# Merging the transfers of y and of the expert biases in a planned two-layer kernel, with a new searched order

## The chip, the cores and the metric

The kernel runs on one core of one Trainium2 chip. The core has five engines that run their own instruction queues: TensorE (PE in the profile, with its weight loads as PEld), VectorE (DVE), ScalarE (ACT), GpSimd (POOL) and SyncE (SP). In this kernel SP does nothing but issue the DMA transfers. Sixteen DMA engines move the data. The metric is the device time of one execution in microseconds (us), as the median of several runs. Before the change it is 741.02 us, from three runs of 740.77 to 742.02 us.

## The reference

What is computed is a chain of six residual blocks on x of shape (8, 256, 128), all in float32. The first and the third block are the same soft mixture of experts (16 experts with 64 slots each); the change touches only what feeds them.

```python
def _L0_ffn_ref(x, norm_g, norm_b, slot_g, slot_b, scale, slot_embeds, Wg, bg, Wu, bu, Wd, bd):
    x = _layernorm(x, norm_g, norm_b)
    se = _layernorm(slot_embeds, slot_g, slot_b) * scale
    logits = jnp.einsum('bnd,esd->bnes', x, se)
    dispatch = jax.nn.softmax(logits, axis=1)
    combine = jax.nn.softmax(logits.reshape(x.shape[0], x.shape[1], -1), axis=-1)
    slots = jnp.einsum('bnd,bnes->besd', x, dispatch)
    gate = jax.nn.gelu(jnp.einsum('besd,edf->besf', slots, Wg) + bg[None, :, None, :], approximate=False)
    up = jnp.einsum('besd,edf->besf', slots, Wu) + bu[None, :, None, :]
    eout = jnp.einsum('besf,efo->beso', gate * up, Wd) + bd[None, :, None, :]
    eout = eout.reshape(eout.shape[0], -1, eout.shape[-1])
    return jnp.einsum('bns,bso->bno', combine, eout)

...
x = x + 0.5 * _L0_ffn_ref(_layernorm(x, axis=-1), ...)
x = x + _L0_attn_ref(_layernorm(x, axis=-1), ...)
x = x + 0.5 * _L0_ffn_ref(_layernorm(x, axis=-1), ...)
x = x + 0.5 * _L1_ffn_ref(_layernorm(x, axis=-1), ...)
x = x + _L1_attn_ref(_layernorm(x, axis=-1), ...)
x = x + 0.5 * _L1_ffn_ref(_layernorm(x, axis=-1), ...)
```

## The kernel before, in words

**How the work is laid out.** The eight batches form two groups of four. For each group the function `group` runs, for two layers: `dispatch` for each of the four batches (the softmax over tokens and the gathering of the slots), `experts` for all four batches together, and then `combine` batch by batch; after the first layer comes `linear`, the linear attention. Then come `glu`, `favor` and `glu` again. So there are 16 dispatches and 4 passes over the 16 experts in all. The second group is planned behind the first by the constant `BEHIND` (L241), so that one group's experts and the other group's dispatches are done at the same time.

**What sets the order.** Nothing is issued at once. Each piece of work is a `Step` with a cost per engine, the cells that it reads and writes, and the buffers that it takes. `Plan.place` (L123) then simulates the engines: among all steps that could start, it takes the one with the earliest start, and breaks ties by a key. The key is shifted part by part by the 202 numbers of `SHIFTS` (L16), which were found by a search. A step is ready when the steps that it needs have ended, plus a latency for the engine (`LAG`, L74; 2000 ns for SP) and an extra `lag` that the step states itself. Buffers are limited: 4 of kind `we` for expert weights, 4 of kind `k4` (which the replicated y uses among others), 10 of kind `comb`. `Plan.issue` (L205) writes the instructions out in the planned order of starts, one queue per engine, so on the chip each engine works through its own fixed list and waits where data are not there. Where the plan finds TensorE idle for over 700 ns, `idle` (L1397) puts in dummy matmuls (L1399), to keep its clock up.

**The work that the change touches.** `replicated` (L573) is called by each dispatch. The gather matmuls (L691) want the normalized y in a layout in which the tokens of one quarter lie on 32 partitions and are repeated on each of the four groups of 32 partitions. To get it, `spill` (L577) writes y to a DRAM tensor `spilled[b]` of shape (32, 8, 128) in four DMAs (L579), one per quarter of the partitions, 32 KB each; `spread` (L584) reads that tensor back four times (L586), 128 KB each, once into each group of 32 partitions. `fetch` (L760) in `experts` loads the weights of one expert into a `we` buffer of 128 rows of 896 numbers: 768 weights (L764, 384 KB), and for every even expert the output biases of this expert and of the next into the last 128 columns, in two DMAs (L767), 32 KB each, every one repeating a row of 128 numbers over 64 partitions. `biased` (L829) adds them after the down projection (L818). A fetch has two conditions: the slots of the third dispatch of its group have been started (`(sl, "in", BG - 2, 0)`), and a `we` buffer is free, which is so when the down projection of an earlier pair of experts has ended.

**Other transfers that the new lengths touch.** `squares_turned` (L440) transposes a tile by way of DRAM: one DMA out (L449) and four DMAs back (L455) that put the 32x32 squares where they belong. Their planned lengths change, not the DMAs.

**The other steps named later.** L615 logits, L632 their running maximum, L649 and L657 the maximum and the exponentials of the dispatch, L670 the division on POOL, L678 the transposes in squares on DVE, L495/L493 the copies of gathered slots into place, L737 and L743 the exponentials for the combination, L787 gate and up projections of the experts, L793 and L798 their activation and product, L859 the combination, L928 to L995 linear attention.

Of the kernel before, what the change touches and what calls it, by code (L numbers as in the profile page):

```python
# [13 lines left out]
P = 128  # L14

SHIFTS = (  # L16
    -2751, -1692, -1691, -12195, -784, -1588, -17523, -441, -1660, -895, -929, -659, -543, -591,
    -517, -633, -219, -357, -610, -370, -144, -340, -138, -261, -103, -124, -149, -112, -87,
    328, -365, -173, -179, -134, 14, 40, -32, 136, -182, -43, -162, -672, 13, -20, 26, 13, -393,
    -13, -49, 76, 108, 25, -337, -106, -98, -405, -124, -14, 106, -15, -91, -232, -26, -141, 72,  # L20
    179, -149, -60, -56, -94, -291, -910, -397, 168, -109, -149, -2, -601, -150, 12, -21, -762,
    -20, -100, 231, -63, -522, -971, -639, -490, -1134, 34, -143, -240, -1126, 30, 98, 272,
    -229, -245, 48, 535, -647, -666, -418, 7, 144, -282, -73, 220, 168, 36, -1118, -353, -720,
    -886, -200, -34, 24, 100, 11, -24, 70, 30, -50, -121, 47, 25, 9, -51, 143, -939, -125, -300,
    -662, -491, -371, -203, -437, -21, -285, -479, -125, 412, 243, 49, 284, 369, 566, -147,
    -339, 157, 267, -173, -269, 162, -518, -492, 53, 116, -414, -523, -222, -451, -400, -304,
    -82, 145, -77, -134, -36, -467, -865, -141, -372, -407, -524, -134, 12, 58, -154, 246, 41,
    -111, 22, 62, -756, -131, 38, -435, -1331, -683, -948, -2046, -2339, -2000, -3450, -2514,
    -3516, -3317, -2307, -1684,
)  # L30


# [184 lines left out]
def macaron_kernel(ctx: ExitStack, tc: tile.TileContext, i: dict, out: bass.AP):  # L217
# [10 lines left out]
    nc = tc.nc  # L228
    B, N, D = out.shape
    TT = N // P  # L230
    NT = B * TT
    E, S, F = 16, 64, 256
# [6 lines left out]
    G, BG = 2, B // 2  # L239
# [16 lines left out]
    step = plan.step  # L256
# [100 lines left out]
    def ps_(*shape):  # L357
        return Buf("ps", (P, *shape))

    def act(n, pointers=False):  # L360
        return 48 + 0.871 * n + 87 * pointers

    def dve(n, extra=0):
        return 58 + 1.07 * n + extra

    def mms(*columns):
        return 6 + sum(2 * max(111.5, 0.8427 * n) for n in columns)
# [72 lines left out]
    def squares_turned(z, n, cells, dst, out):  # L440


        flat = lambda: z()
        there = dram.tile([P, n // 32, 32], F32, tag=f"t{len(turns)}", name=f"t{len(turns)}")
        turns.append(there)
        step({"DVE": 58 + 1.07 * n}, lambda _: nc.vector.transpose(z(), z()), cells, cells)

        def spill(_):
            nc.sync.dma_start(there.rearrange("p k j -> p (k j)"), z())  # L449


        def place(_):
            squares = there.rearrange("(a i) (t f) j -> f i t a j", a=4, f=4)
            for f in range(4):
                nc.sync.dma_start(  # L455
                    dst()[32 * f : 32 * f + 32].rearrange("p (t a j) -> p t a j", a=4, j=32),
                    squares[f],
                )

        step({"SP": 475}, spill, cells, [there.name], lag=1.5 * n)  # L460
        step({"SP": 2000}, place, [there.name], out, lag=2.5 * n)

    turns = []

# [106 lines left out]
    spilled = [dram.tile([32, N // 32, D], F32, tag=f"y{b}", name=f"y{b}") for b in range(B)]  # L571

    def replicated(y, b):  # L573

        yr = Buf("k4", (P, N // 32, D))

        def spill(_):  # L577
            for k in range(4):
                nc.sync.dma_start(  # L579
                    spilled[b].rearrange("i (t k) d -> i k t d", k=4)[:, k],  # L580
                    y.ap[32 * k : 32 * k + 32],
                )

        def spread(_):  # L584
            for a in range(4):
                nc.sync.dma_start(yr.ap[32 * a : 32 * a + 32], spilled[b])  # L586

        step({"SP": 2500}, spill, [(y, t) for t in range(TT)], [("y", b)], lag=-1500)
        step({"SP": 1765}, spread, [("y", b)], [yr], lag=900)
        return yr  # L590


# [1 line left out]
    def dispatch(b, sl):  # L594
# [4 lines left out]
        y = norm(b, True)  # L599
        yt = transposed(y, TT, True)  # L600
        yr = replicated(y, b)
        if not loaded:
            key, plan.key = plan.key, 60000
# [145 lines left out]
    def experts(sl):  # L749
        def whole(j):  # L750
            return [(sl, j, q) for q in range(BG)]

        filled = [(sl, "in", q, a) for q in range(BG) for a in range(4)]

        def eo():
            return sl.ap.rearrange("p j k b s -> p j (k b s)").rearrange(
                "p j (b n) -> p j b n", n=2 * S1
            )

        def fetch(e):  # L760
            we = Buf("we", (P, 6 * P + D))

            def run(_):
                nc.sync.dma_start(we.ap[:, 0 : 6 * P], i["We"][e])  # L764
                if e % 2 == 0:
                    for k in range(2):
                        nc.sync.dma_start(  # L767
                            we.ap[S * k : S * k + S, 6 * P :],
                            i["bd"][e + k].partition_broadcast(S),
                        )  # L770

            step(
                {"SP": 475 if e % 2 else 1400}, run, [(sl, "in", BG - 2, 0)], [we],
                lag=1900 if e % 2 else 1000,
            )
            return we

        def front(e, we):
            j, k = e // 2, e % 2
            ht = Buf("k2", (P, 2, BG * S))  # L780
            for c in range(2):
                pe = ps_(2, BG * S)
                ga = Buf("k1", (P, BG * S))

                def hidden(_, c=c, pe=pe):
                    for m in range(2):
                        mm(  # L787
                            pe.ap[:, m, :], we.ap[:, ts(2 * m + c, P)],
                            sl.ap[:, j, k, :, 0:S], start=True, stop=True,
                        )  # L790

                def gate(_, c=c, pe=pe, ga=ga):
                    nc.scalar.activation(  # L793
                        ga.ap, pe.ap[:, 0, :], AF.Gelu, bias=bg[:, e, c : c + 1]
                    )

                def up(_, c=c, pe=pe, ga=ga):
                    nc.vector.scalar_tensor_tensor(  # L798
                        ht.ap[:, c, :], pe.ap[:, 1, :], bu[:, e, c : c + 1], ga.ap,
                        ALU.add, ALU.mult,  # L800
                    )

                step(
                    {"PE": mms(256, 256)}, hidden, [we, *whole(j), *filled], [pe], takes=[ga, (ht, c)]
                )
                step({"ACT": act(256, True)}, gate, [pe], [ga], table="gelu")
                step({"DVE": dve(256, 59)}, up, [pe, ga], [(ht, c)])
            return ht

        def back(j, wes, hts):  # L810

            po = ps_(BG, P)

            def down(_):
                for q in range(BG):
                    for c in range(2):
                        for k in range(2):
                            mm(  # L818
                                po.ap[S * k : S * k + S, q, :], hts[k].ap[:, c, ts(q, S)],
                                wes[k].ap[:, ts(4 + c, P)], start=(c == 0), stop=(c == 1),  # L820
                                tile_position=(0, S * k),
                            )

            step(
                {"PE": 1880}, down,
                [*wes, *((ht, c) for ht in hts for c in range(2))], [po],
            )

            def biased(_):  # L829
                nc.vector.tensor_tensor(  # L830
                    eo()[:, j, :, 0:D], po.ap,
                    wes[0].ap[:, 6 * P :].unsqueeze(1).to_broadcast([P, BG, D]), ALU.add,
                )

            step({"DVE": dve(512)}, biased, [wes[0], po], whole(j))

            def twos(_):
                nc.gpsimd.memset(eo()[:, j, :, D : D + 1], 2.0)

            step({"POOL": 65}, twos, [], whole(j))  # L840

        got = []
        for e in range(E):
            plan.part()
            we = fetch(e)
            got.append((we, front(e, we)))
            if e % 2 == 0 and e:
                back(e // 2 - 1, *zip(*got[e - 2 : e]))
        back(NJ - 1, *zip(*got[E - 2 :]))
        return eo  # L850
# [631 lines left out]
```

## Time and profile before

| what | value |
|---|---|
| median of 3 runs | 741.02 us |
| the profiled execution itself | 743.85 us |
| its span, from the first to the last instruction | 742.1 us |
| mean granted TensorE clock | 0.998 |
| PE busy | 728.8 us, 98% |
| DVE busy | 517.2 us, 70% |
| ACT busy | 410.7 us, 55% |
| POOL busy | 306.1 us, 41% |
| DMA, 16 engines, hardware queue | 61.36 MB in 102032 packets, 30.6% |

The profiled execution is 2.8 us longer than the median of the timed runs, and 1.75 us of it lie outside the span. PE is the engine with the most work; its idle time is small and lies at particular places, which is why windows of the trace tell more here than shares of the span. In the window tables each row gives a stretch of the span, its length, the busy time and the number of instructions of the five engines (PE, PEld, DVE, ACT, POOL), the granted clock (1.00 is full speed), the busy share of the 16 DMA engines and what they moved in GB/s. In a timeline a row gives the start, the time, the engine, the line, the operation, the tiles and a count, and in brackets how long the engine sat idle before it and what ended that.

### The profile page before, as it was taken

Reading aid. Unit: us, or ns where it says so; the run is one execution under the profiler, and the core shown is the slowest. Engines: PE = TensorE matmul, PEld = TensorE weight load, DVE = VectorE, ACT = ScalarE, POOL = GpSimd, SP = SyncE. Lnnn points to the kernel's source line nnn. Section 1 sums busy time; section 2 is a strip of 40 time slices with the busy share of each in tenths; the row PEclk is TensorE's granted clock in tenths of the full one; section 3 lists DMA queues with packets and bytes.
Section 4 is the critical chain, followed back from the end, with each engine's and each line's share of the span. In section 5 each row is a group of like instructions: output and inputs, shape, how many; then the busy total and the mean of one; then the engine's idle time right before and its main releaser. Section 6 shows DMA issues by size and latency. Waiting matters only on the chain.

```text
span 742.1 us, 15296 instructions
## 1 busy us (share of the span) xinstructions
PE 728.8 (98%) x5814; PEld 609.5 (82%) x5814; DVE 517.2 (70%) x1103; ACT 410.7 (55%) x774; POOL 306.1 (41%) x419
## 2 busy tenths in 40 slices
PE   8999999998999999999999999999999999999998
PEld 7878888997889988889878879788687677878787
DVE  6999965577868798975564274455998978855442
ACT  4889967257665577884553240433555664363331
POOL 7989446133427752459910022000745545211000
PEclk9999999999999999999999999999999999999999
DMA  5553432333330526333631210200344244120100
GB/s 143 150 140 118 139 93 94 109 81 97 126 114 2 146 83 197 99 94 119 171 99 52 85 29 1 57 0 15 78 114 95 42 118 81 32 60 14 42 1 29
DMA packets 102105, 62.34 MB, mean 84 GB/s; under 512 B 73104, under 2 KB 88848, under 8 KB 102032
## 3 DMA queue, kind: packets, MB, share of 16 engines
q1 hardware_dynamic: 102032, 61.36, 30.6%
q8 instruction: 46, 0.75, 0.4%
q14 instruction: 27, 0.22, 0.1%
HBM read 49.80 MB, written 11.53 MB: 83 GB/s over the span
## 4 chain that ended last, share of the span: by engine, by line
PE 87%; DVE 5%; DMA 3%; SPq 2%; issue 1%; POOL 1%; ACT 1%; POOLq 0%
PE ps L1077 27%; PE ps L787 14%; PE ps L818 8%; PE ps L859 8%; PE ps L691 6%; PE ps L615 4%; PE ps L1177 4%; PE ps L1147 4%; PE ps L1150 4%; PE ps L375 2%; DMA we<-in_We 1%; PE ps L1256 1%; DVE k L632 1%; PE ps L1307 1%; PE ps L1341 1%; PE ps L907 1%
## 5 line engine op out<-in xcount | busy, mean ns | idle before, releaser
L787 PE MATMUL ps<-slots,we 128*128 128x256 f32 x512 | 121.8, 384 | 4.0 <-DMA we<-in_We 2.3
L787 PEld LDWEIGHTS ps<-slots,we 128*128 128x128 f32 x512 | 94.7, 191 | 20.1 <-issue 5.2
L1077 PE MATMUL ps<-comb,slots 128*128 128x256 f32 x448 | 103.1, 381 | 0.0
L1077 PE MATMUL ps<-comb,comb 128*128 128x256 f32 x448 | 102.5, 381 | 0.0
L1077 PEld LDWEIGHTS ps<-comb,slots 128*128 128x128 f32 x448 | 83.6, 190 | 15.4 <-issue 3.9
L1077 PEld LDWEIGHTS ps<-comb,comb 128*128 128x128 f32 x448 | 83.6, 190 | 13.6 <-issue 2.5
L737 POOL TENSOR_TENSOR comb<-comb,k 128x1024 f32<-128x1024 f32 x32 | 75.1, 2369 | 33.5 <-DVE k L384 14.0
L793 ACT ACTIVATE k<-ps,small 128x256 f32<-128x256 f32 x128 | 56.5, 475 | 48.4 <-PE ps L787 46.1
L382 ACT COPY k<-ps 128x512 f32<-128x512 f32 (+2 forms) x55 | 28.5, 519 | 93.8 <-PE ps L1077 83.1
L670 POOL TENSOR_TENSOR comb<-comb,sm 128x1024 f32<-128x1024 f32 x32 | 60.9, 1911 | 41.4 <-DVE sm L665 41.4
L798 DVE SCALAR_TENSOR_TENSOR k<-ps,small,k 128x256 f32<-128x256 f32 x128 | 57.2, 475 | 29.2 <-ACT k L793 28.5
L412 POOL TENSOR_SCALAR sm<-sm 128x2 f32<-128x2 f32 x52 | 10.0, 193 | 153.1 <-DVE sm L406 140.1
L657 ACT ACTIVATE comb<-comb,sm 128x256 f32<-128x256 f32 x128 | 63.3, 497 | 13.7 <-PE ps L691 7.4
L1091 DVE TENSOR_TENSOR comb<-ps,k 128x512 f32<-128x512 f32 x48 | 32.9, 687 | 49.0 <-PE ps L1077 25.5
L818 PEld LDWEIGHTS ps<-we,k 128*64 128x64 f32 x1024 | 55.3, 137 | 9.2 <-issue 4.7
L615 PE MATMUL ps<-k,seT 128*128 128x256 f32 x256 | 61.7, 383 | 0.8 <-DVE k L495 0.5
L818 PE MATMUL ps<-we,k 128*64 128x128 f32 x1024 | 62.2, 275 | 0.0
L691 PE MATMUL ps<-comb,k 32*128 32x256 f32 x1024 | 59.9, 380 | 0.1
L859 PEld LDWEIGHTS ps<-slots,comb 128*128 128x128 f32 x512 | 58.4, 192 | 1.5 <-issue 1.3
L859 PE MATMUL ps<-slots,comb 128*128 128x129 f32 x512 | 59.6, 276 | 0.0
L1099 ACT ACTIVATE comb<-comb 128x512 f32<-128x512 f32 x48 | 30.0, 629 | 51.0 <-DVE comb L1091 50.8
L691 PEld LDWEIGHTS ps<-comb,k 32*128 32x128 f32 x1024 | 51.4, 185 | 5.6 <-issue 1.4
(144 smaller groups left out, 1303.7 us busy)
## 6 DMA issues: line engine op xcount, KB each, us to landing
we<-in_We SPq DMA_DIRECT2D x64, 384.0 KB, 3.8
k<-y SPq DMA_DIRECT2D x64, 128.0 KB, 2.9
t<-comb SPq DMA_DIRECT2D x8, 512.0 KB, 2.8
k<-t SPq DMA_DIRECT2D x32, 128.0 KB, 3.5
y<-k SPq DMA_DIRECT2D x64, 32.0 KB, 1.9
we<-in_bd SPq DMA_DIRECT2D x64, 32.0 KB, 3.6
t<-k SPq DMA_DIRECT2D x16, 128.0 KB, 1.7
k<-t SPq DMA_DIRECT2D x64, 32.0 KB, 2.3
```

Source lines behind the costliest of these rows:

```text
L615: mm(pl.ap[:, j, :], seT[:, 2 * u + j].rearrange("p k s -> p (k s)"), yt.ap, start=True, stop=True,)
L657: nc.scalar.activation(ex.ap[:, 4 * h + j, :], comb.ap[:, 4 * h + j, :], AF.Exp, bias=mx.ap[:, j : j + 1], accum_out=mx.ap[:, 4 + j : 5 + j],)
L670: nc.gpsimd.tensor_tensor(ex.ap[:, part], ex.ap[:, part], mx.ap[:, 8:12].unsqueeze(2).to_broadcast([P, 4, N]), ALU.mult,)
L691: mm(po.ap, yr.ap[rows, c, :], ex.ap[rows, :, 32 * c : 32 * c + 32], start=(c == 0), stop=(c == N // 32 - 1), tile_position=(32 * a, 0),)
L737: nc.gpsimd.tensor_tensor(raw, raw, mb.ap.unsqueeze(1).to_broadcast([P, 4, N]), ALU.subtract)
L787: mm(pe.ap[:, m, :], we.ap[:, ts(2 * m + c, P)], sl.ap[:, j, k, :, 0:S], start=True, stop=True,)
L793: nc.scalar.activation(ga.ap, pe.ap[:, 0, :], AF.Gelu, bias=bg[:, e, c : c + 1])
L798: nc.vector.scalar_tensor_tensor(ht.ap[:, c, :], pe.ap[:, 1, :], bu[:, e, c : c + 1], ga.ap, ALU.add, ALU.mult,)
L818: mm(po.ap[S * k : S * k + S, q, :], hts[k].ap[:, c, ts(q, S)], wes[k].ap[:, ts(4 + c, P)], start=(c == 0), stop=(c == 1), tile_position=( ...
L859: mm(po.ap[:, t, 0 : D + 1], comb.ap[:, j, ts(t, P)], eo()[:, j, q, 0 : D + 1], start=(j == 0), stop=(j == NJ - 1),)
L1077: mm(bank.ap[:, o], w(k)[:, c, ts(o, P)], rhs().rearrange("p (c n) -> p c n", c=2)[:, c, :], start=(start and o + c == 0), stop=(stop and ...
L1091: nc.vector.tensor_tensor(C(i, k)(), bank.ap.rearrange("p o n -> p (o n)"), other(), ALU.add)
```

## The change

The four spill DMAs of a dispatch become one, and so do the four of its spread; the one spread reads the spilled tensor with a repeated outermost dimension of 4. The biases of a pair of experts are put on the host beside the weights of the even expert, already repeated over the partitions, so that the even expert's fetch is one DMA of 896 columns (448 KB) and the odd one's is one of 768 (384 KB); the DMAs of L767 are gone. The planner's lengths for the transfers are set anew, for the squares' DMAs too, and with them the 202 shifts. The arithmetic is unchanged.

```diff
 SHIFTS = (
-    -2751, -1692, -1691, -12195, -784, -1588, -17523, -441, -1660, -895, -929, -659, -543, -591,
...
-    -3516, -3317, -2307, -1684,
+    -1108, -978, -978, -7284, -465, -1049, -1056, 14, 3, -9, -90, -47, -662, 147, 106, 93, -161,
...
+    -196, -658, -498, 325,
 )
...
-        step({"SP": 475}, spill, cells, [there.name], lag=1.5 * n)
-        step({"SP": 2000}, place, [there.name], out, lag=2.5 * n)
+        step({"SP": 335}, spill, cells, [there.name], lag=1.1 * n - 850)
+        step({"SP": 2400 + 0.7 * n}, place, [there.name], out, lag=1.2 * n - 300)
...
         def spill(_):
-            for k in range(4):
-                nc.sync.dma_start(
-                    spilled[b].rearrange("i (t k) d -> i k t d", k=4)[:, k],
-                    y.ap[32 * k : 32 * k + 32],
-                )
+            nc.sync.dma_start(spilled[b].rearrange("i (t k) d -> k i t d", k=4), y.ap)
 
         def spread(_):
-            for a in range(4):
-                nc.sync.dma_start(yr.ap[32 * a : 32 * a + 32], spilled[b])
-
-        step({"SP": 2500}, spill, [(y, t) for t in range(TT)], [("y", b)], lag=-1500)
-        step({"SP": 1765}, spread, [("y", b)], [yr], lag=900)
+            nc.sync.dma_start(
+                yr.ap, spilled[b].unsqueeze(0).to_broadcast([4, 32, N // 32, D])
+            )
+
+        step({"SP": 475}, spill, [(y, t) for t in range(TT)], [("y", b)], lag=-500)
+        step({"SP": 475}, spread, [("y", b)], [yr], lag=900)
...
+            n = 6 * P if e % 2 else 6 * P + D
+            at = (6 * P + D) * (e % 2)
+
             def run(_):
-                nc.sync.dma_start(we.ap[:, 0 : 6 * P], i["We"][e])
-                if e % 2 == 0:
-                    for k in range(2):
-                        nc.sync.dma_start(
-                            we.ap[S * k : S * k + S, 6 * P :],
-                            i["bd"][e + k].partition_broadcast(S),
-                        )
-
-            step(
-                {"SP": 475 if e % 2 else 1400}, run, [(sl, "in", BG - 2, 0)], [we],
-                lag=1900 if e % 2 else 1000,
-            )
+                nc.sync.dma_start(we.ap[:, 0:n], i["We"][e // 2][:, at : at + n])
+
+            step({"SP": 475}, run, [(sl, "in", BG - 2, 0)], [we], lag=1500)
...
+    bd = np.repeat(get(f0 + "bd").reshape(-1, 2, P), P // 2, axis=1)
...
+        "We": np.concatenate([we[0::2], bd, we[1::2]], axis=2),
```

## The prediction

> **What bounds the kernel now.** I read first the busy line, then windows, because PE is busy 98% of the span and only its idle places can be won.
>
> ```profile
> PE 728.8 (98%) x5814; PEld 609.5 (82%) x5814; DVE 517.2 (70%) x1103; ACT 410.7 (55%) x774; POOL 306.1 (41%) x419
> ```
>
> ```profile
> core 0: us, PE busy (x) PEld busy (x) DVE busy (x) ACT busy (x) POOL busy (x), PEclk, DMA share, GB/s
> 0.00:62.00 62.00, 56.86 (x479) 47.64 (x479) 55.40 (x123) 44.73 (x123) 55.10 (x90) 1.00 0.59 158
> 62.00:180.15 118.15, 116.67 (x1081) 102.94 (x1079) 88.01 (x197) 81.67 (x163) 52.57 (x62) 1.00 0.32 95
> 180.15:186.50 6.35, 4.18 (x16) 3.48 (x16) 3.00 (x6) 3.67 (x7) 2.55 (x3) 0.73 0.50 114
> 186.50:300.00 113.50, 112.13 (x1030) 98.52 (x1029) 93.57 (x217) 77.17 (x161) 54.71 (x78) 1.00 0.38 110
> 300.00:739.00 439.00, 438.99 (x3216) 356.87 (x3214) 276.78 (x562) 203.44 (x325) 141.14 (x188) 1.00 0.25 64
> ```
>
> From 300 us on PE never stops. Before, it stands 1.5 us in the second row, 2.2 in the third, 1.4 in the fourth; the first 62 us hold 5.1 us of idling and 12.7 us of dummy matmuls (the same window for L1399 alone), with DVE and POOL at 55 of 62 us: the start hangs on DVE and POOL, not on transfers. In the third row the clock falls to 0.73; from 183.0 to 186.5 it is 0.51, so the stop also cost 6.35 x 0.27 = 1.7 us in slow matmuls. The queue of SP and the timeline of PE show why PE stood:
>
> ```profile
> 168.02 3.04 SPq L579 DMA_DIRECT2D y<-k  x4
> 171.56 2.58 SPq L455 DMA_DIRECT2D k<-t  x4
> 174.24 0.55 SPq L764 DMA_DIRECT2D we<-in_We  x1
> 174.83 1.16 SPq L767 DMA_DIRECT2D we<-in_bd  x2
> 176.03 0.58 SPq L764 DMA_DIRECT2D we<-in_We  x1
> ```
>
> ```profile
> 175.79 0.68 PE L928 MATMUL ps<-WqkvT,k 128*128 128x128 f32 x4 [0.32 <-DMA k<-t]
> ...
> 182.32 1.46 PE L787 MATMUL ps<-slots,we 128*128 128x256 f32 x4 [2.17 <-DMA we<-in_We]
> ```
>
> Four spill issues, four square issues and two bias issues stand ahead of the second fetch of weights; it is issued at 176.03, takes 6.2 us and lands when PE starts again. The stop of 1.17 us at 104.2 is put down to ACT, yet the fetch issued at 99.32 took 5.9 us and landed at 105.3, just before PE went on at 105.39: a fetch too.
>
> **The sum's base.** The profiled execution took 743.85 us, 742.1 of span and 1.75 around it; the median is 741.02. I add changes to 741.0.
>
> **What is removed.** Issue times by the views of the tiles (medians): 48 spill DMAs at 593 ns, 48 spreads at 420, 64 bias DMAs at 588: 28.5 + 20.2 + 37.6 = 86 us of SP. Almost all of it is hidden: SP waits far longer for others (112.4 us at L764 for the down projections that free the buffers). If that cover went, SP's list would still be the shorter one. It counts where a fetch waits behind issues:
> - At 104.2: two bias issues (1.10 us) stood between the fetches; the late one goes out 1.1 earlier. Gain 1.2 with its share of the queue.
> - At 175.5: the squares go out some 2.4 us earlier (3.04 of spills become 0.6). Gain 0.3.
> - At 180.15: 2.4 earlier for the spills and 1.2 for the biases, against 2.17 of stop. Gain 2.2, and 1.7 of slow clock.
>
> Together 5.4 us. The added 128 columns of an even fetch are the bytes that the biases moved anyway (64 x 32 KB), so they cost nothing new; if not hidden, 64 KB at 18 GB/s for each of 16 engines is 0.2 us per fetch.
>
> [...]
>
> **What the two single transfers cost.** No row has a transfer whose outermost dimension counts four; all in the table of issues count 32 or more. Of it:
>
> ```profile
> k<-y SPq DMA_DIRECT2D x64, 128.0 KB, 2.9
> t<-comb SPq DMA_DIRECT2D x8, 512.0 KB, 2.8
> ...
> y<-k SPq DMA_DIRECT2D x64, 32.0 KB, 1.9
> ```
>
> ```profile
> 50.00:60.00 10.00, 8.92 (x95) 7.01 (x89) 9.90 (x17) 8.51 (x23) 9.30 (x5) 1.00 0.85 245
> ```
>
> 245 GB/s at a share of 0.85 are 18 GB/s per engine. The spread's 524288 bytes take 1.8 us on sixteen engines and 7.3 on four; a spill's 131072 take 0.46 or 1.8. The rest of an old piece is 1.8 us (1.9 less 0.11 for 32 KB) and 2.4 (2.9 less 0.46). So the new spill lands after 2.3 or 3.6 us, the spread after 4.2 or 9.7. I take the slow end of each: the nearest thing by shape is the old piece, and the new outermost step goes over four such pieces; if the work is shared out along that step, four engines move one piece each.
>
> [...]
>
> The planner reckons 0.475 + 1.5 = 1.98 us and 0.475 + 2.9 = 3.38. Queued behind SP's spread, which has to wait for the spill, stands whatever SP holds next. Are the gathers late? The first dispatch spills at 8.67 and gathers at 27.34: 18.7 us, where 3.6 + 9.7 = 13.3 are needed (8.2 before). Not late; the softmax in between covers it. If that cover went, the gather on PE would be late by what is missing. The fetches behind a spread have less cover:
>
> ```profile
> 206.84 1.84 SPq L586 DMA_DIRECT2D k<-y  x4
> 208.85 0.35 SPq L764 DMA_DIRECT2D we<-in_We  x1
> 209.38 2.67 SPq L586 DMA_DIRECT2D k<-y  x4
> 212.09 0.42 SPq L764 DMA_DIRECT2D we<-in_We  x1
> ```
>
> - Place one: the fetches of 208.85 and 212.09 took 5.8 and 4.8 us, and PE stood 0.15 and 0.18 us for them; it has no slack. With the spills short but landing after 3.6 us (201.6 to 205.2), the spreads start 1.6 us earlier and move until 206.84 - 1.6 + 2 x 7.3 = 219.8. The second fetch, 3.2 us alone (that of 97.79), lands 7.7 + 3.2 = 10.9 after its issue, 6.1 later than now. With one slow-clock stretch, 7.8.
> - Place two: a spread at 284.91 and a fetch at 286.67, which took 4.7 us; PE stood 0.35 us at 291.20. The spill (from 280.15) lands at 283.75, so the spread starts 1.1 earlier and moves until 291.1: the fetch lands 4.4 + 3.2 = 7.6 after its issue, 2.9 later; with the clock 4.6.
>
> Both places belong to the old order. The bounds for the new are 0 (no fetch near a spread) and 12.4 (both). I take the first fully and the second half: 7.8 + 2.3 = 10.1.
>
> **The order.** What 202 shifts are worth no row shows. Below, it can win at most the rest of the idling and the dummies of the start after PE's first real matmul at 7.84 (some 10 us); above, it can lose as much. Since the start hangs on DVE and POOL, whose work is the same, I take 0. The squares' new lengths change no DMA; their plan for 256 numbers goes from 7.5 to 6.4 us (0.335 + 1.43 + 2.58 + 2.01), still above 1.7 + 1.9 + 2.3 = 5.9 by the rows, so 0, and their issue delays are in the places above.
>
> **Sum.** 741.0 - 5.4 + 10.1 = 745.7.
>
> **Rivals.**
> - *The spread is as wide as its pieces were: faster.* One mechanism: a spread moves in 1.8 us, no fetch is held up, and the 5.4 us are won: 741.0 - 5.4 = 735.6. For it: 512 KB of t<-comb land in 2.8 us. Against it: that transfer counts 128 at its outermost, not four. It decides if a spread lands within about 5 us.
> - *Slow, but covered: no change.* The new order lays its fetches away from the spreads but for one stop of 3.7 us and its clock: 741.0 - 5.4 + 5.4 = 741.0. For it: three of the eight spreads after 62 us have no fetch within 7.3 us behind them. Against it: the planner reckons with 3.38 us, so nothing in its plan keeps fetches away.
> - *It doesn't do what it says.* The single DMAs are cut into four again, SP issues as before, and only the biases are gone: 1.2 at 104 and 1.2 at 180: 738.6. Nothing in the profile speaks for it; the diff has one call each.
>
> **How the numbers follow.** Forecast 0.52, wide rival 0.30, covered 0.13, cut again 0.05. Forecast's own range 742.5 (one stop with its clock, 6.9) to 753 (both places whole, 748.0, and a start 5 us longer, half of the order's bound). Wide rival 734 to 739. The range 735 to 753 leaves out about a tenth at each end. 0.2% (1.5 us) is what a measurement can tell from no change: faster 0.30 + 0.05 = 0.35, same 0.11 of the covered case, slower 0.52 + 0.02 = 0.54.
>
> **What would show it.** Spread: about 9.7 us to landing if the step is right, under 5 if wrong. Spill: 3.6 or 2.3. PE: waits for we<-in_We of several us between 160 and 300, within 10 us after a spread, with the clock at 0.5 behind them. The stops at 104 and 180 gone. From 300 on PE at 100% as before; if it isn't, the new order is the cause and the sum is wrong there. A first L787 far from 61.57 would show that the start moved.

## The result, and the profile after

The changed kernel takes 821.38 us in the median of four runs (820.84 to 824.84), against 740.89 for the kernel before on the same chip. The ratio is 1.1096 with a 95% interval of 1.1061 to 1.113: 80 us slower. The forecast was 745.7 within 735 to 753, so the direction was right and the size far off.

The page's first part, after: busy time, share of the span and number of instructions of each engine.

```profile
span 819.4 us, 15073 instructions
...
PE 741.7 (91%) x5804; PEld 620.0 (76%) x5804; DVE 518.1 (63%) x1105; ACT 425.8 (52%) x788; POOL 308.9 (38%) x416
```

The span has grown by 77.3 us. PE's busy time has grown by 12.9 us. Nearly all of that lies in two groups whose matmuls ran in part at a low clock: the experts' gate and up projection (6.1 us more, 401 ns for a matmul in the mean where it was 384; the granted clock reads 0.74 from 99 to 105 us, behind the longest stop) and the gather (5.9 us more, 409 ns where it was 380; 0.69 from 45 to 49 us, 0.75 from 66 to 70). PE's idle time has grown from 13.3 to 77.7 us. The windows of the changed kernel, with the columns as in the prediction, show where:

```profile
core 0: us, PE busy (x) PEld busy (x) DVE busy (x) ACT busy (x) POOL busy (x), PEclk, DMA share, GB/s
0.00:70.00 70.00, 59.97 (x460) 50.48 (x460) 52.58 (x117) 42.40 (x116) 50.74 (x89) 0.90 0.36 91
70.00:99.00 29.00, 0.71 (x3) 0.58 (x3) 4.68 (x5) 3.84 (x10) 1.74 (x1) 0.58 0.44 107
99.00:230.00 131.00, 130.16 (x1208) 114.90 (x1206) 90.79 (x209) 87.31 (x166) 56.32 (x70) 0.99 0.32 99
230.00:260.00 30.00, 13.91 (x57) 10.55 (x54) 9.34 (x22) 8.18 (x17) 8.43 (x5) 0.72 0.39 96
260.00:328.00 68.00, 67.08 (x669) 60.43 (x669) 57.18 (x134) 46.40 (x102) 38.70 (x49) 1.00 0.29 68
328.00:380.00 52.00, 35.05 (x297) 29.38 (x297) 29.58 (x65) 27.51 (x61) 22.67 (x27) 0.86 0.43 112
380.00:816.00 436.00, 434.69 (x3121) 353.66 (x3120) 273.57 (x556) 210.13 (x319) 130.33 (x176) 1.00 0.23 61
```

Row 2 is one long stop of 28.3 us, just ahead of the first experts. Rows 4 and 6 hold 16.1 and 17.0 us more, and row 1 holds 10.0. From 380 us on PE stands only 1.3 us in all, so it works there nearly as it did before from 300 on. So the loss lies in the stretch in which y is spilled and spread. What PE waited for, in total, times and longest (us):

```profile
PE ps L777 <- DMA we<-in_We: 62.1, 8, 28.3
PE ps L687 <- DMA k<-y: 7.3, 2, 4.5
```

L777 is the experts' gate and up projection (L787 before), L687 the gather (L691 before). PE waits for weights, although the change left fewer DMAs for their fetches. SP's list shows why they came late:

```profile
31.16 0.54 SPq L580 DMA_DIRECT2D k<-y  x1
31.80 0.53 SPq L577 DMA_DIRECT2D y<-k  x1
42.52 0.51 SPq L580 DMA_DIRECT2D k<-y  x1
43.12 0.53 SPq L577 DMA_DIRECT2D y<-k  x1
52.42 0.51 SPq L580 DMA_DIRECT2D k<-y  x1
53.02 0.53 SPq L577 DMA_DIRECT2D y<-k  x1
63.05 0.51 SPq L580 DMA_DIRECT2D k<-y  x1
63.65 0.53 SPq L577 DMA_DIRECT2D y<-k  x1
73.63 0.51 SPq L580 DMA_DIRECT2D k<-y  x1
...
85.79 1.93 SPq L763 DMA_DIRECT2D we<-in_We  x4
```

Each pair is a spread and the next dispatch's spill, and between a spill and its spread SP stands for some 10 us: it has to wait for the spill to land. The first spill, with nothing else of y under way, took 3.5 us (8.70 to 12.20). The later ones were issued right behind a spread and took 9 to 11, as the chain of work that ended last shows (start, time, what):

```profile
43.12 9.25 DMA y<-k
...
53.02 9.96 DMA y<-k
...
63.65 9.94 DMA y<-k
...
74.20 10.95 DMA y<-k
...
85.79 12.44 DMA we<-in_We
```

The trace's records of single packets show the queuing itself: of the spill issued at 31.80 the first packet moves at 38.85, when the packets of the spread ahead of it (32.48 to 40.50) run out. The first fetch of weights stands behind all these pairs: 85.79 where it was 53.51. So of the stop of 28.3 us, which begins at 70.1, 15.7 us pass before that fetch is issued, and 12.6 until PE can use it. Before the change the first fetch landed 5.1 us after its issue.

SP was late already ahead of these lines. The second spill went out at 27.56, where the kernel before had it at 18.02: behind the first spread one issue of a constant (s, at 15.70) held SP for 4.23 us, where it took 0.58 before, and then SP stood 5.2 us more until that spread had landed.

In SP's table of waits the standing at the spreads is the line

```profile
SPq L580 <- DMA y<-k: 90.6, 15, 10.1
```

(4.7 us before). And while a spread moves, the windows of the changed kernel read:

```profile
33.00:39.00 6.00, 3.83 (x25) 3.23 (x24) 5.76 (x9) 5.93 (x18) 5.69 (x10) 1.00 0.24 76
45.00:49.00 4.00, 4.00 (x41) 3.32 (x34) 0.89 (x2) 0.57 (x1) 0.00 (x0) 0.69 0.25 82
```

The last two columns tell it: the sixteen DMA engines are busy to 0.24 and 0.25, which is what four of sixteen would give, and they move 76 to 82 GB/s. The records of single packets, which name no engine, agree with the four: in these two windows exactly four packets are under way for 92% and 93% of the time, and five or six for the rest. The 524288 bytes of a spread take 524288 / 82 GB/s = 6.4 us at that pace. From its issue to its landing a spread takes longer: the gather that waited for the spread of 31.16 went on at 41.34, and the one that waited for that of 52.42 at 61.83, so 10.2 and 9.4 us.

### The profile page after: what moved, and what is told of

It reads as the page before. It is cut to its first block, busy times and chain, and to the rows that moved or that the text cites. A ratio compares the mean times of both kernels' runs of the same rounds, so it can differ in the third digit from the quotient of the medians.

```text
span 819.4 us, 15073 instructions
## 1 busy us (share of the span) xinstructions
PE 741.7 (91%) x5804; PEld 620.0 (76%) x5804; DVE 518.1 (63%) x1105; ACT 425.8 (52%) x788; POOL 308.9 (38%) x416
## 4 chain that ended last, share of the span: by engine, by line
PE 62%; DMA 17%; DVE 6%; POOL 6%; ACT 5%; issue 2%; SPq 1%; POOLq 0%; DVEq 0%; ACTq 0%
PE ps L1067 22%; PE ps L777 10%; DMA y<-k 10%; DMA we<-in_We 6%; PE ps L849 6%; PE ps L808 4%; PE ps L1167 3%; PE ps L1140 3%; PE ps L1137 3%; PE ps L687 3%; POOL comb L666 2%; ACT comb L653 2%; POOL k L419 1%; POOL sm L413 1%; ACT comb L739 1%
## 5 line engine op out<-in xcount | busy, mean ns | idle before, releaser
L777 PE MATMUL ps<-slots,we 128*128 128x256 f32 x512 | 127.9, 401 | 62.1 <-DMA we<-in_We 62.1
L777 PEld LDWEIGHTS ps<-slots,we 128*128 128x128 f32 x512 | 99.9, 202 | 80.0 <-DMA we<-in_We 35.2
L1067 PEld LDWEIGHTS ps<-comb,slots 128*128 128x128 f32 x448 | 83.2, 191 | 15.7 <-issue 4.2
L687 PE MATMUL ps<-comb,k 32*128 32x256 f32 x1024 | 65.8, 409 | 7.3 <-DMA k<-y 7.3
L381 ACT COPY k<-ps 128x512 f32<-128x512 f32 (+2 forms) x52 | 26.4, 510 | 86.6 <-PE ps L1067 64.8
L687 PEld LDWEIGHTS ps<-comb,k 32*128 32x128 f32 x1024 | 56.2, 202 | 14.1 <-DVE comb L674 5.0
```

The lines of the kernel that those rows point to most:

```text
L687: mm(po.ap, yr.ap[rows, c, :], ex.ap[rows, :, 32 * c : 32 * c + 32], start=(c == 0), stop=(c == N // 32 - 1), tile_position=(32 * a, 0),)
L777: mm(pe.ap[:, m, :], we.ap[:, ts(2 * m + c, P)], sl.ap[:, j, k, :, 0:S], start=True, stop=True,)
L1067: mm(bank.ap[:, o], w(k)[:, c, ts(o, P)], rhs().rearrange("p (c n) -> p c n", c=2)[:, c, :], start=(start and o + c == 0), stop=(stop and ...
```

## The experiments

Theory W: a merged transfer of y runs on four DMA engines, the next spill and the fetches queue on the same four, and SP stands in between. Theory O: the new order and the shortened lengths are bad in themselves. Two narrower theories stood against parts of W: S, that any single DMA of 512 KB from a repeated source is slow, whatever its outermost count; and H, that the harm is SP standing at the spread and not the loaded engines. All times are medians, with ratios to the kernel before on the same chip.

**Four pieces again, in the changed order (e1).**

```diff
-            nc.sync.dma_start(spilled[b].rearrange("i (t k) d -> k i t d", k=4), y.ap)
+            for k in range(4):
+                nc.sync.dma_start(
+                    spilled[b].rearrange("i (t k) d -> i k t d", k=4)[:, k],
+                    y.ap[32 * k : 32 * k + 32],
+                )
...
-            nc.sync.dma_start(
-                yr.ap, spilled[b].unsqueeze(0).to_broadcast([4, 32, N // 32, D])
-            )
+            for a in range(4):
+                nc.sync.dma_start(yr.ap[32 * a : 32 * a + 32], spilled[b])
```

> The changed kernel with y's spill and spread as four DMAs each again; planner lengths, shifts, order and the merged fetch of weights and biases stay as changed. Theory W (a merged transfer of y runs on four DMA engines only, the next spill queues behind it on the same four, and SP stands in between, so the fetches of weights go out late): the 80 us vanish, 733 to 745 us, no PE stop over 3 us for the weights. Theory O (the new order and the shortened lengths are bad in themselves): 800 us or more stay. If both matter, a time in between gives their shares.

752.62 us, ratio 1.0162 (1.0148 to 1.0175). Of the 80 us, 69 are gone with nothing changed but the number of DMAs of y. 12 remain, more than W had said (733 to 745 in all, no stop over 3 us); the longest PE stop is 5.4 us at the first experts.

**One transfer each, but wide, with an outermost count of 128 (e8).**

```diff
+    def flat_of(b):
+        return spilled[b].rearrange("i n d -> (i n d)").rearrange("(p c) -> p c", p=P)
...
-            nc.sync.dma_start(spilled[b].rearrange("i (t k) d -> k i t d", k=4), y.ap)
+            nc.sync.dma_start(flat_of(b), y.ap.rearrange("p t d -> p (t d)"))
...
-            nc.sync.dma_start(
-                yr.ap, spilled[b].unsqueeze(0).to_broadcast([4, 32, N // 32, D])
-            )
+            nc.sync.dma_start(
+                yr.ap.rearrange("p (r m) d -> p r (m d)", r=4),
+                flat_of(b).unsqueeze(1).to_broadcast([P, 4, TT * D]),
+            )
```

> The changed kernel with one spill and one spread as changed in number and bytes, but laid out so that the outermost dimension counts 128 on both sides: the spill writes 128 contiguous rows, the spread reads each of 128 rows and repeats it four times inside. The tokens stand in the wrong places of the replicated y, so the gathered slots are not the reference's; the work is the same. Theory W: spill about 2.0 us, spread about 4 us, 733 to 742 us in all. Theory S (one large transfer with a repeated source is slow because of its size or the repetition, whatever its outermost dimension): the spread stays at 7 us or more, 800 us or more in all.

742.56 us, ratio 1.0032 (1.0017 to 1.0048). The table of issues (count, KB each, median us to landing) and a window in which a spread moves:

```profile
k<-y SPq DMA_DIRECT2D x16, 512.0 KB, 4.0
```

```profile
23.00:25.50 2.50, 2.50 (x15) 2.18 (x16) 2.50 (x5) 1.73 (x4) 2.42 (x4) 1.00 0.78 258
```

The same 512 KB, in one DMA, from a repeated source, land in 4.0 us at a DMA share of 0.78, with up to 20 packets under way at once. So neither the size nor a repeated source as such nor the number of DMAs makes the transfer slow, and theory S falls. What is left is the outermost count of four. In e8 the repetition also is no longer the outermost step, and no run separates the two for the spread; that the count decides is supported by the spill, which repeats nothing: while the changed kernel's first one moves (10.2 to 11.7 us), the share is 0.27, and it landed after 3.5 us, where e8's first one, issued at 8.65, landed by 10.36, after 1.7.

The time was just above the 733 to 742 that W expected, and the spills' median of 3.5 us above its 2.0.

**The merged y alone, in the old order (e3):** the same two edits to y as in the change, on the kernel before.

> The kernel before, with its order and lengths, and only y's spill and spread merged as in the change. Theory W: most of the loss appears without any new order, 775 to 830 us, with spreads about 10 us apart on SP in the first 90 us and the first expert matmul 15 to 30 us later than 61.6. Theory O: within 745 us.

780.21 us, ratio 1.0537 (1.0519 to 1.0554). SP's list in this kernel:

```profile
47.63 2.05 SPq L581 DMA_DIRECT2D k<-y  x2
49.77 11.46 SPq L578 DMA_DIRECT2D y<-k  x3
62.69 2.05 SPq L581 DMA_DIRECT2D k<-y  x2
64.79 0.94 SPq L761 DMA_DIRECT2D we<-in_We  x2
```

No new order is needed for the loss, so O cannot be all. But the same two edits to y cost 40 us in the old order and 69 in the new (the change against e1): here the first fetch goes out at 64.79, the first expert matmul follows at 79.92, and the longest stop is 17.1 us. The old plan gave the transfers of y more time on SP; that this is the room that made the loss smaller is argued, no run changes it alone.

**Which of the two transfers (e6, e7).** e6 is the changed kernel with only the spread in four, e7 with only the spill in four (the edits are those of e1, one at a time).

> The changed kernel with only the spread as four DMAs again; the spill stays one DMA with an outermost dimension of four. Which of the two transfers carries the loss? If it is the spread's 6.5 us on four engines, behind which the next spill queues: 750 to 760 us (as with four pieces of both, 752.6, plus 1.6 us per spill where that shows). If it is the spill: 800 us or more.

> The changed kernel with only the spill as four DMAs again; the spread stays one DMA with an outermost dimension of four. If the spread on four engines carries the loss, the four spills also queue behind it with their share on those engines: 790 to 830 us. If the single spill carries it: 750 to 760 us.

e6: 745.56 us, ratio 1.0075 (1.0054 to 1.0096), better than expected. e7: 814.1 us, 1.0993 (1.0972 to 1.1014). The spread carries the loss. Against a wide spill the four-engine spill costs some 3.4 us (742.12 of e2 below, whose spread is cut differently too). And e6 is 7.1 us faster than e1, from which it differs in the spill alone: in this order one spill on four engines is better than four pieces. In e1 the four issues hold SP for 2.5 us or more, in e6 the one for 0.5; that this makes the difference is not shown.

**Is it SP that stands, or the engines' queues? (e9, e10).**

```diff
-        step({"SP": 475}, spill, [(y, t) for t in range(TT)], [("y", b)], lag=-500)
-        step({"SP": 475}, spread, [("y", b)], [yr], lag=900)
+        step({"SP": 475}, spill, [(y, t) for t in range(TT)], [("y", b)], lag=8000)
+        step({"SP": 475}, spread, [("y", b)], [yr], lag=7200)
```

e10 has these lags and the wide transfers of e8.

> The changed kernel with its DMAs as they are, but the planner told that a spill lands 10.5 us after its issue and a spread 9.7 (extra lags of 8000 and 7200 ns). SP then gets the spread later in its list and the fetches of weights stand ahead of it. The order is not searched for these lengths, so it may cost something by itself; the next run has the same order with wide transfers and is the yardstick. Theory H (SP standing at a spread, with the fetches behind it, carries most of the loss): within 15 us of the next run. Theory Q (the queues of the four engines hold the fetches even where SP doesn't stand): 30 us or more above it.

> The yardstick of the run before: the same long lengths for the planner and the same order, with one spill and one spread whose outermost dimension counts 128 (the replicated y holds the tokens in the wrong places, so the gathered slots are not the reference's). If the untuned order costs little, 742 to 755 us; what it is above 742.6 is the price of the order planned for long transfers.

e9: 825.07 us, 1.1141 (1.1124 to 1.1157). e10: 776.28 us, 1.0476 (1.0451 to 1.0501), more than expected, so the untuned order alone costs 34 us over e8 (41.4 us of PE's time in e10 are dummy matmuls for planned idling, 11.2 in e8). The two waits of e9, SP's first:

```profile
SPq L580 <- DMA y<-k: 6.1, 2, 4.3
```

```profile
PE ps L777 <- DMA we<-in_We: 29.5, 4, 12.6
```

SP's standing at the spreads is down from 90.6 to 6.1 us, and yet e9 is 49 us above e10, 27 of them in PE's waits for weights (29.5 us against 2.3). Theory H falls for this order. The first fetch shows what else holds PE: in e9 it is issued at 66.36 and used at 83.72, 17.4 us later; in e10 it takes 5.9 us (58.67 to 64.61). From 69 to 72 us the packet records of e9 have mostly sixteen packets under way; from 75 to 83.7, while PE stands, mostly four, at a DMA share of 0.25 to 0.27, and among them are packets of a spread (4096 bytes) and the last ones of the fetches (3072 and 3584 bytes). So the last packets of a fetch move among those of a spread, mostly four at a time, and the fetch has landed only when they are through.

SP isn't wholly free in e9: single issues take long (a spread's 6.18 us at 47.03, a fetch's 7.44 at 334.13). And what part SP's standing has in the changed kernel as a whole stays open, because the order of e9 is another; in its longest stop, 15.7 of the 28.3 us pass before the fetch is issued.

**The fetch alone, in the old order (e4):** the change's `fetch` and its layout of weights and biases, on the kernel before.

> The kernel before, with its order and lengths, and only the biases laid beside the weights: one DMA per fetch. Prediction's terms: the stop at 104.2 goes (1.2 us), of the stop at 180 the part that two bias issues make (1.2 us) and perhaps its slow clock (1.7): 737 to 740 us. Rival: the longer even fetch and its larger rows hold up the odd fetch as much as the biases did: 741 us, no change.

739.77 us, ratio 0.9986 (0.9977 to 0.9995): a gain of some 0.7 us, at the upper end of the 737 to 740 expected. In its profile the stops at 104 and 180 us are gone.

**Wide transfers that keep the layout (e5, e2).** The spill of e8, and four spreads that pick the chunks, in the old order with the merged fetch (e5) and in the changed order (e2).

```diff
-            nc.sync.dma_start(
-                yr.ap, spilled[b].unsqueeze(0).to_broadcast([4, 32, N // 32, D])
-            )
+            for a in range(4):
+                nc.sync.dma_start(
+                    yr.ap[32 * a : 32 * a + 32].rearrange("p (k m) d -> p k (m d)", k=4),
+                    flat_of(b).rearrange("(k i) c -> i k c", k=4),
+                )
...
-                        po.ap, yr.ap[rows, c, :], ex.ap[rows, :, 32 * c : 32 * c + 32],
+                        po.ap, yr.ap[rows, TT * (c % 4) + c // 4, :], ex.ap[rows, :, 32 * c : 32 * c + 32],
```

> A version meant to keep what the change was after: order and lengths of the kernel before, one fetch per expert with the biases inside, y's spill as one DMA of 128 contiguous rows, y's spread as four DMAs that pick 1 KB runs (outermost dimension 32), and the gather reading the chunks in the new order. Theory W: no transfer of y on fewer than sixteen engines, so no stop appears; SP has 48 spill issues less than before. 737 to 740 us, at or below the run with the merged fetch alone (739.8). Rival: the spread's 1 KB runs (512 descriptors for a spread in place of 128) hold the fetches up: 741 us or more.

> The same spill of 128 rows and four spreads of 1 KB runs in the changed kernel's new order, with its lengths. Between the run with one wide transfer each (742.6) and the one with a narrow spill and four spreads (745.6): 742 to 746 us. If it lies below 740, the new order is worth something once the transfers are wide; if above 741, the new order is no better than the old one.

e5: 737.37 us, ratio 0.9957 (0.9943 to 0.9971), 3.2 us below the kernel before on the same chip. e2: 742.12 us, 1.0019 (1.001 to 1.0028). The DMAs of the two are the same, so the new order and lengths cost 4.8 us. e5's windows:

```profile
62.00:180.00 118.00, 117.81 (x1090) 104.23 (x1089) 88.95 (x201) 82.83 (x164) 53.55 (x63) 1.00 0.33 102
180.00:300.00 120.00, 119.11 (x1067) 105.67 (x1066) 101.52 (x230) 85.01 (x181) 61.89 (x83) 1.00 0.36 108
```

Of the 5.0 us of idling that the kernel before had between 62 and 300 us, 1.1 are left, and the clock reads 1.00 in both rows.

**A search for that version (e11):** e5 with lengths read from its own trace (those of the squares' DMAs are set anew too), and the shifts searched for them.

```diff
-        step({"SP": 2500}, spill, [(y, t) for t in range(TT)], [("y", b)], lag=-1500)
-        step({"SP": 1765}, spread, [("y", b)], [yr], lag=900)
+        step({"SP": 335}, spill, [(y, t) for t in range(TT)], [("y", b)], lag=-500)
+        step({"SP": 1700}, spread, [("y", b)], [yr], lag=700)
...
-            step(
-                {"SP": 475 if e % 2 else 1400}, run, [(sl, "in", BG - 2, 0)], [we],
-                lag=1900 if e % 2 else 1000,
-            )
+            step({"SP": 430}, run, [(sl, "in", BG - 2, 0)], [we], lag=2200)
```

> The version with one spill of 128 rows, four spreads and the merged fetch, with the planner's lengths taken from that version's own trace (spill 335 ns on SP and 1.5 us more, spread 1.7 and 2.7, fetch 0.43 and 4.2) and the 202 shifts searched for these lengths. If true lengths and a search are worth what the change hoped, it lies below the old order's 737.4: 733 to 737 us. If the old order with its generous lengths is as good: 737 to 740. If a searched order is fragile whatever its lengths, above 741.

752.53 us, ratio 1.017 (1.0156 to 1.0184): the third branch. Its windows show 10 us of idling where e5 has 0.9, and no single wait makes it: the largest groups of PE's waits in the whole run are 3.9 us for the squares (k<-t), 3.2 and 3.0 for DVE and 2.5 for weights.

```profile
180.00:300.00 120.00, 109.97 (x1019) 97.29 (x1017) 97.42 (x217) 84.02 (x169) 56.79 (x70) 1.00 0.31 90
```

## Why the prediction was wrong in size

- *The base* (741.0) held: 740.89.
- *What is removed* (5.4 us): the places were right, the size too large. The merged fetch alone brought 0.7 and with the short spill 3.2 us (e4, e5). The stops were those of one profiled execution that was 2.8 us longer than the median; that the timed runs have smaller stops is argued, not shown.
- *What the two single transfers cost*: the slow end was the right one. Spill 3.6 us forecast, 3.5 measured where nothing else of y was under way; spread 9.7 forecast, 10.2 and 9.4 measured (the first one, beside loads of constants, some 13: 12.20 to 25.17); four engines, shown by the share of 0.25 and by four packets at a time; 18 GB/s per engine assumed, 82 / 4 = 20 measured. That the work is shared out along the outermost step was the author's supposition. Four packets at a time for a count of four and e8's share of 0.78 for a count of 128 agree with it, and no run varies the spread's count alone.
- *"Not late; the softmax in between covers it"* is the step that failed, and with it the price list of two places. It set the 13.3 us of the first dispatch against its own gather, as if each dispatch had the engines to itself. But the eight dispatches of the start follow each other, and their transfers queue: a spill behind a spread takes 10 us where it takes 3.5 alone, SP's list stands at each, and the first fetch moves from 53.51 to 85.79. Two gathers do come late, by 7.3 us in all, but the larger price is the fetches behind them: the first expert matmul starts at 98.36 where it was 61.57, after 28.3 us of stop in one place. The prediction's sum had nothing for the start, and its range 5 us, because "the start hangs on DVE and POOL, not on transfers". This was true of the kernel before, and it was a statement about a cover of 3 us: there the first fetch landed 5.1 us after 53.51 and was used at 61.57. The windows at 230 and 328 show the later chains, 33 us where 10.1 were priced.
- *The clock*: each stop was given one slow stretch of 1.7 us. PE's busy time grew by 12.9 us, which is several such stretches; the mean granted clock fell from 0.998 to 0.954, in part while PE stood. Nor does the length of a stop alone decide: behind 2.17 us in the kernel before, the clock read 0.51 (183.0 to 186.5), but in e11 PE stood 3.03 us up to 250.43 and the granted clock from 240 to 260 still reads 1.00.
- *The order*, taken as 0, costs 4.8 us with equal transfers (e2 against e5) and about 40 with narrow ones (e3, 780.2, against the change, 821.4, which also has the merged fetch). That the plan's shorter lengths took out the room that the old ones had left is the likely reason; no run shows it apart from the new shifts.
- *The rivals*: the wide spread, priced at 735.6, is measured as 742.56 in the new order (e8). Of the 7 us between them the order makes 4.8 (e2 against e5); most of the rest is that less was won than the 5.4 us. The other two fall with the traces: the fetches are held up 62.1 us, and the changed kernel has 16 spread DMAs of 512 KB, so nothing was cut again.

## What to carry to other kernels

Before several DMAs are merged into one, look at the outermost count of both access patterns: here the four spread transfers of 32 rows became one with an outermost count of four, which moved at a DMA share of 0.24 to 0.25, four packets at a time, where the one of e8 with a count of 128 moved at 0.78, and fewer issues on SP were no match for that. For the spill, with a quarter of the bytes, it went the other way: one narrow spill beat four pieces by 7 us in the same order (e6 against e1). Such a slow transfer held up the wide ones behind it, too: the first fetch took 17.4 us from issue to use in e9 and 5.9 in e10, which has the same lengths and shifts and the wide transfers of e8. So price it for the whole chain of transfers and issues behind it, not against its own consumer alone. And lengths in a hand-made plan that look too long may be the room that keeps the order robust: setting them anew with a new search was a loss here both times, by 4.8 us (e2 against e5) and by 15 (e11 against e5). Longer ones without a search were a loss too (e10).

## What the runs showed that was not expected

A spill of 128 KB that lands in 3.5 us alone lands in 10 behind a spread that moves at a share of 0.28 (53.02 to 62.98; the share from 55.5 to 59). One broadcasting read of 512 KB that moves at 0.78 (e8) lands in 4.0 us, no more than its four pieces need with issues of 0.42 us each and 2.9 us to landing. And two plans of this kernel with nearly the same work, e5 and e11, lie 15 us apart, though PE has 725.7 and 728.8 us of work in them. Last, one spill on four engines was faster than four spills, by 7 us.
